# When results are read back, where the next pair's products begin, and how K products stand between scores, in a fused cross-attention and FFN kernel

## The chip, the cores and the metric

The kernel runs on one core of a Trainium2 chip. The metric is the device time of one execution in microseconds (us), the median of several runs. All data are fp32.

## The reference, cut to what matters

```python
# x (8,128,512), ctx (8,128,512); 32 heads of 128; INTER = 1376
h   = rmsnorm(layernorm(x)) * lnw
q, k, v = h @ w_q.T, ctx @ w_k.T, ctx @ w_v.T          # each (8,128,32,128)
score = einsum('bqhd,bkhd->bhqk', q, k) + position_bias
score = where(mask, score, -inf); p = where(mask, softmax(score), 0)
attn  = einsum('bhqk,bkhd->bqhd', p, v).reshape(8,128,4096)
x = x + layernorm(x) + attn @ w_out.T
n = layernorm(x)
x = x + ((silu((n @ Wg.T) * ag) * ((n @ Wu.T) * au)) @ Wd.T) * ad
```

## The kernel before

Every large product is done in seven half-size products instead of eight (the Strassen-Winograd form): a 2x2 block product needs seven products of blocks and of sums of blocks. `sums_a` (L222 to L225) and `sums_b` (L230 to L233) form the four sums of a left and of a right operand, each by four vector operations. The sums of weights are done by GpSimd (POOL), those of tokens and of attention results mostly by VectorE (DVE).

The program has these stages: K and V of head group 0, the Q products of all groups (queries go to DRAM), eight attention groups `g` of four heads, the output product, and the FFN (`mm_f` L916, `d` L995). The change lies in the attention stage and in the start of the output product.

**One attention step** (g, b) handles batch b, all four heads of the group:

- POOL adds the position bias and the mask into `s` (L332); the product of scores goes into the PSUM tile `sc` (L337, 8 matmul rows of the profile for four heads).
- DVE adds them (L340), takes the maximum (L342) and its negative `nmx` (L344); ScalarE (ACT) takes four exponentials with row sums (L347); DVE forms the reciprocal (`ri`, L354, L355), multiplies (L356), and transposes 32x32 blocks into `tt` (L372).
- SyncE's DMA queue (SP) writes `turned` (L374) to DRAM and reads it back as `pT` in four transfers (L379).
- Three steps later (`advance(3)`) TensorE (PE) multiplies `pT` with V into `av` (L395), ACT copies it to `aT` (L400), and ACT's DMA queue stores it in `att[g][b // 2]` (L401).

**Between the scores.** While group g's steps run, TensorE's remaining time goes to the K and V products of group g+1. They come from the generator `products` (`kv`, `project_T` L296, `project_V` L314, both through `seven`): each `next(products)` gives one product of one half (`t` = 0 or 1), followed by a copy on ACT (L270, L280) or an add on DVE (L275, L286) that takes the result out of its bank. The order of the seven is 2, 1, 6, 7, 4, 5, 3. Products 1, 6, 7 and 4 of one half share a bank, and each waits until the result of the one ahead is out. In group 0 three products stand ahead of the first scores, and then three or four between steps.

**The last group** (g = 7) has no next group. What is left of V's products is done in its first step, and from then on the output product of pair 0 (batches 0 and 1) stands between the scores: in step b the attention results `a` of group b are read back (`attended`, L608: on POOL's DMA queue for pair 0, on SP's for later pairs), DVE forms their sums `S_a`, and `out_products` multiplies with output weights `wo` of that group (L627, seven products, 28 matmul rows of the profile). `load_wo` fetches these weights (L588, L589, L596; 1 MB each on SP), and POOL forms their sums `T_o` right after. After the last step the remaining two `av` sets run, then pairs 1 to 3 of the output product, each in four PSUM banks.

**What sets the order.** A scheduler orders the instructions of each engine by its own estimates. What is issued through `InOrder` stays in the written order among its own kind; in the profile such instructions stand under L45. Until now that is TensorE in steps (0,0) to (0,3), TensorE and VectorE in the whole last group, and some other places. `acts` (18 slots of 4 KB per partition, tag "a"), `work`, `wpool` and `spool` hold the tiles, and a tile waits for the release of its slot. PSUM has two banks each for `sc`, `av`, `mm` (K and V products, later the first two out banks) and `pt`.

Of the kernel before, what the change touches and what calls it, by code (L numbers as in the profile page):

```python
# [10 lines left out]
F32 = mybir.dt.float32  # L11
U8 = mybir.dt.uint8
AF = mybir.ActivationFunctionType
ALU = mybir.AluOpType
# [3 lines left out]
P = 128  # L18
# [31 lines left out]
def xattn_ffn_kernel(  # L50
# [19 lines left out]
    nc = tc.nc  # L70
    B, S, D = x.shape
# [4 lines left out]
    GH = 4  # L76
    NG = H // GH
# [5 lines left out]
    HC = DC // 2  # L83
# [144 lines left out]
    def sums_b(eng, b11, b12, b21, b22, t1, t2, t4, eng3=None):  # L228

        eng.tensor_tensor(t1, b12, b11, SUB)  # L230
        eng.tensor_tensor(t2, b22, t1, SUB)
        (eng3 or eng).tensor_tensor(b12, b22, b12, SUB)
        eng.tensor_tensor(t4, b21, t2, SUB)  # L233
        return {1: b11, 2: b21, 3: b22, 4: t4, 5: t1, 6: t2, 7: b12}
# [89 lines left out]
        yield from seven(name, range(2), product, part, *banks)  # L324


    def probabilities(g, b, qT, kT, pb, between=None):

        cols = bass.ts(b, S)
        n = f"{g}_{b}"  # L330
        s = work.tile([P, GH, S], F32, tag="s", name=f"s_{n}", bufs=3)
        nc.gpsimd.tensor_tensor(  # L332
            s, pb, mneg[:, b : b + 1, :].to_broadcast([P, GH, S]), ALU.add
        )
        sc = ps.tile([P, GH, S], F32, tag="sc", name=f"sc_{n}")
        for j in range(GH):
            tensor.matmul(  # L337
                sc[:, j, :], qT[:, j, bass.ts(b % 2, S)], kT[j][:, cols], start=True, stop=True
            )
        vector.tensor_tensor(s, sc, s, ALU.add)  # L340
        mx = small.tile([P, GH], F32, tag="mx", name=f"mx_{n}")
        vector.tensor_reduce(mx, s, AX.X, ALU.max)  # L342
        nmx = small.tile([P, GH], F32, tag="nmx", name=f"nmx_{n}")
        vector.tensor_scalar(nmx, mx, FLOOR, -1.0, ALU.max, ALU.mult)  # L344
        sm = small.tile([P, GH], F32, tag="sm", name=f"sm_{n}")
        for j in range(GH):
            (InOrder(tc, nc.scalar) if (g, b) == (0, 0) else nc.scalar).activation(  # L347
                s[:, j, :], s[:, j, :], AF.Exp,
                bias=nmx[:, j : j + 1], accum_out=sm[:, j : j + 1],
            )  # L350
        if between:
            between()
        ri = small.tile([P, GH], F32, tag="ri", name=f"ri_{n}")
        vector.tensor_scalar_max(ri, sm, TINY)  # L354
        vector.reciprocal(ri, ri)  # L355
        vector.tensor_tensor(  # L356
            s, s, ri.unsqueeze(2).to_broadcast([P, GH, S]), ALU.mult
        )
        return s
# [46 lines left out]
    def advance(lag):  # L406
        while len(pend) > lag:
            attend(*pend.pop(0))
# [172 lines left out]

    def load_wo(g):
        src = woT[bass.ts(g, GW), :].rearrange("(c p) n -> p c n", p=P)
        if g == NG - 1:
            up, dn, t12, t4 = (
                acts.tile([P, 2, D], F32, tag="a", name=f"wo{g}_{k}") for k in range(4)
            )
            nc.sync.dma_start(up, src[:, :HC])  # L588
            nc.sync.dma_start(dn, src[:, HC:])  # L589
            t1, t2, t4 = (  # L590
                t.rearrange("p (c n) -> p c n", c=HC) for t in (t12[:, 0], t12[:, 1], t4[:, 0])
            )
        else:
            held = g in (2, 3, 4)
            w = (wpool if held else wos).tile([P, GH, D], F32, tag="w", name=f"wo{g}")
            nc.sync.dma_start(w, src)  # L596
            t = (spool if held else wos).tile(
                [P, 3, HC, HW], F32, tag="S" if held else "T", name=f"T_o{g}"
            )
            up, dn, t1, t2, t4 = w[:, :HC], w[:, HC:], t[:, 0], t[:, 1], t[:, 2]  # L600
        wo_t[g] = sums_b(
            nc.gpsimd, up[:, :, :HW], up[:, :, HW:], dn[:, :, :HW], dn[:, :, HW:], t1, t2, t4
        )

    def attended(g, i):
        a = acts.tile([P, 2, GH, S], F32, tag="a", name=f"a_{g}_{i}")

        (nc.sync if i else nc.gpsimd).dma_start(a, att[g][i])  # L608
        s = acts.tile([P, 3, HC, S], F32, tag="a", name=f"S_a{g}_{i}")
        return sums_a(  # L610
            vector, a[:, 0, :HC], a[:, 0, HC:], a[:, 1, :HC], a[:, 1, HC:],
            s[:, 0], s[:, 1], s[:, 2],
        )

    def by_product(banks):
        return {n: banks[k // 2][:, k % 2, :] for k, n in enumerate((1, 2, 6, 7, 4, 5, 3))}

    def out_products(i, order, banks, fetched):

        m = by_product(banks)  # L620
        for at, g in enumerate(order):
            sa = fetched.pop(g)
            if i and at + 1 < NG:
                fetched[order[at + 1]] = attended(order[at + 1], i)
            for k, n in enumerate((1, 2, 6, 7, 4, 5, 3)):
                for c in range(HC):
                    tensor.matmul(  # L627
                        m[n], sa[n][:, c, :], wo_t[g][n][:, c, :],
                        start=(g == order[0] and c == 0 and k % 2 == 0),
                        stop=(g == order[-1] and c == HC - 1), skip_group_check=True,  # L630
                    )
            yield


# [14 lines left out]
    for g in range(NG):  # L649
        kT, v = kvs.pop(g)  # L650
        pb = biases.pop(g)
        if g + 1 < NG:
            biases[g + 1] = load_bias(g + 1)
        if g + 2 < NG:
            kv_w[g + 2] = load_kv(g + 2)
        if g + 1 < NG:
            products = kv(g + 1, kvs)
        if g in (1, 2):
            load_wo(g - 1)
        if g == NG - 2:  # L660
            load_wo(2)
        if g == NG - 1:
            tensor, vector = InOrder(tc, nc.tensor), InOrder(tc, nc.vector)
            fetched = {}
        for b in range(B):
            if b % 2 == 0:
                qT = ahead.pop((g, b // 2))
                at = todo.index((g, b // 2)) + 2
                if at < len(todo):
                    ahead[todo[at]] = load_queries(*todo[at])  # L670

            if (g, b) == (0, 0):
                tensor = kv_tensor = InOrder(tc, nc.tensor)
                for _ in range(3):
                    next(products)
            if g == NG - 1:

                p = probabilities(
                    g, b, qT, kT, pb, lambda: fetched.update({b: attended(b, 0)})
                )  # L680
            else:
                p = probabilities(g, b, qT, kT, pb)
            pend.append((g, b, transpose_p(g, b, p), v))
            advance(3)

            if (g, b) != (0, 0):
                for _ in range(4 if b % 2 and (g < NG - 2 or b == 3) else 3):
                    next(products, None)
            if (g, b) == (0, 3):
                tensor = kv_tensor = nc.tensor  # L690
            if g == NG - 1:
                if b == 0:
                    proj.close()
                    wos = pools(outp)("wosB", 2, reuse_waits="tile")

                    first_banks = [
                        pl.tile([P, 2, HW], F32, tag=tag, name=f"m{k}_0")
                        for k, (pl, tag) in enumerate(2 * [(ps_mm, "mm")] + 2 * [(ps_tp, "pt")])
                    ]
                    first_out = out_products(0, list(range(NG)), first_banks, fetched)  # L700
                if b < NG - 4 or b == 5:
                    load_wo(b + 3 if b < NG - 4 else NG - 1)
                if b:
                    next(first_out)
    advance(2)
    next(first_out)
    advance(0)
    fetched[0] = attended(0, 1)
    tensor, vector = nc.tensor, nc.vector
    attn.close()  # L710


# [68 lines left out]
    for i in range(1, B // 2):  # L781
        last = i + 1 == B // 2
        order = [2, 3, 4, 5, 6, 7, 0, 1] if last else list(range(NG))
        banks = [ps.tile([P, 2, HW], F32, tag="m", name=f"m{k}_{i}") for k in range(4)]
        if i > 1:
            fetched[order[0]] = attended(order[0], i)
        for n, _ in enumerate(out_products(i, order, banks, fetched)):
            if n in (2, 3):
                norm2_T(*ys[n - 2])
        m = by_product(banks)  # L790
        first_residual(i)
        if last:
            outp.close()
            wts.close()
        else:
            residual(i, x1[i], m, banks)
            ys = norm2(i, x1[i])
# [276 lines left out]
```

## Time and profile before

| | |
|---|---|
| median of 3 runs | 1118.73 us (1117.19 to 1122.49) |
| profiled execution | 1120.01 us, span 1118.2 us |
| mean granted TensorE clock | 0.997 |
| PE busy | 1093.8 us, 98% of the span |
| POOL, DVE, ACT busy | 373.7, 571.4, 314.1 us |
| first attention group (first K product to first V product of the next group) | 247.33 to 282.81 us |
| last group, and pair 1 to its third group of heads | 682.72 to 781.59 us |

All times within the program are counted from the start of the span of the profiled execution. In a timeline row the first number is the start, the second the length of a group of instructions of one kind that follow each other, then engine, line, operation, output and inputs, shape and count; a bracket holds the idle time of the engine just before it and what released it. Matmuls are pipelined, so that rows that follow each other overlap a little. A table by stretches gives, for each stretch, its length, the busy time and number of instructions of PE, PEld (weight loads), DVE, ACT and POOL, then the granted clock of TensorE, the DMA engines' busy share and GB/s.

### The profile page before, as it was taken

Reading aid. Unit: us, or ns where it says so; the run is one execution under the profiler, and the core shown is the slowest. Engines: PE = TensorE matmul, PEld = TensorE weight load, DVE = VectorE, ACT = ScalarE, POOL = GpSimd, SP = SyncE. Lnnn points to the kernel's source line nnn. Section 1 sums busy time; section 2 is a strip of 40 time slices with the busy share of each in tenths; the row PEclk is TensorE's granted clock in tenths of the full one; section 3 lists DMA queues with packets and bytes.
Section 4 is the critical chain, followed back from the end, with each engine's and each line's share of the span. In section 5 each row is a group of like instructions: output and inputs, shape, how many; then the busy total and the mean of one; then the engine's idle time right before and its main releaser. Section 6 shows DMA issues by size and latency. Waiting matters only on the chain.

```text
span 1118.2 us, 13138 instructions
## 1 busy us (share of the span) xinstructions
PE 1093.8 (98%) x4526; PEld 775.1 (69%) x4526; DVE 571.4 (51%) x1122; ACT 314.1 (28%) x880; POOL 373.7 (33%) x386
## 2 busy tenths in 40 slices
PE   7999999998999999999999999998999999999998
PEld 4656666654868778685968778887888864444687
DVE  4664444436555565555555666643444333434732
ACT  2422211114444443434444344221000012223100
POOL 5283335535333333322311733620000316930010
PEclk9999999999999999999999999998999999999999
DMA  9113344448555555556545557664222512110011
GB/s 284 51 38 113 113 155 183 151 177 275 171 161 173 168 177 169 179 181 187 167 157 178 168 179 237 225 213 156 94 86 84 188 59 76 38 38 0 1 38 38
DMA packets 117538, 154.44 MB, mean 138 GB/s; under 512 B 12032, under 2 KB 71680, under 8 KB 117472
## 3 DMA queue, kind: packets, MB, share of 16 engines
q1 hardware_dynamic: 104416, 128.95, 36.2%
q10 hardware_dynamic: 11408, 18.88, 4.8%
q0 software_dynamic: 1648, 5.77, 1.6%
q8 instruction: 36, 0.59, 0.2%
q14 instruction: 30, 0.25, 0.1%
HBM read 101.14 MB, written 52.43 MB: 137 GB/s over the span
## 4 chain that ended last, share of the span: by engine, by line
PE 88%; DMA 4%; DVE 3%; POOL 2%; issue 1%; ACT 1%; SPq 0%; ACTq 0%; POOLq 0%; DVEq 0%
PE mm_v L314 16%; PE mm_k L296 14%; PE m L627 13%; PE mm_f L916 10%; PE mm_q L485 9%; PE d L995 6%; PE av L395 4%; PE sc L337 4%; PE ia_q L541 3%; PE ib_q L541 2%; PE mm_q L296 2%; DMA wo<-in_woT_dram 2%; DMA a<-att 1%; PE mm_k L45 1%; DMA wv<-in_wvT_dram 1%
## 5 line engine op out<-in xcount | busy, mean ns | idle before, releaser
L332 POOL TENSOR_TENSOR s<-pb,mneg 128x512 f32<-128x512 f32 x64 | 81.4, 1275 | 274.1 <-DVE tt L372 228.9
L314 PE MATMUL mm_v<-wv,ctx_sb 128*128 128x256 f32 x512 | 118.2, 379 | 1.4 <-DMA wv<-in_wvT_dram 1.4
L296 PE MATMUL mm_k<-ctx_sb,wk 128*128 128x512 f32 x224 | 105.0, 602 | 6.5 <-DMA wk<-in_wkT_dram 4.4
L347 ACT ACTIVATE s<-s,nmx 128x128 f32<-128x128 f32 x252 | 98.0, 390 | 44.6 <-DVE nmx L344 29.5
L314 PEld LDWEIGHTS mm_v<-wv,ctx_sb 128*128 128x128 f32 x512 | 94.5, 190 | 14.4 <-DMA wv<-in_wvT_dram 2.2
L314 PE MATMUL mm_v<-S_v,ctx_sb 128*128 128x256 f32 x384 | 86.6, 380 | 3.3 <-DVE v L45 1.7
L400 ACT COPY aT<-av 128x512 f32<-128x512 f32 x64 | 37.5, 587 | 183.2 <-PE av L395 142.1
L314 PEld LDWEIGHTS mm_v<-S_v,ctx_sb 128*128 128x128 f32 x384 | 71.9, 190 | 14.1 <-DVE v L45 2.3
L296 PE MATMUL mm_k<-ctx_sb,S_k 128*128 128x512 f32 x168 | 75.1, 592 | 0.0
L627 PE MATMUL m<-wo,a 128*128 128x256 f32 x300 | 74.3, 386 | 0.0
L337 PEld LDWEIGHTS sc<-k,q 128*128 128x128 f32 x416 | 58.7, 191 | 20.2 <-issue 18.2
L340 DVE TENSOR_TENSOR s<-sc,s 128x512 f32<-128x512 f32 x56 | 38.7, 691 | 65.3 <-PE sc L337 61.1
L296 PEld LDWEIGHTS mm_k<-ctx_sb,wk 128*128 128x128 f32 x224 | 40.4, 193 | 44.4 <-issue 34.8
L493 ACT COPY q<-mm_q 128x512 f32<-128x512 f32 x56 | 31.4, 588 | 121.5 <-PE mm_q L485 111.8
L627 PEld LDWEIGHTS m<-wo,a 128*128 128x128 f32 x300 | 57.6, 194 | 7.8
L545 DVE TENSOR_TENSOR q<-q,ia_q 128x256 f32<-128x256 f32 x84 | 34.9, 421 | 52.6 <-PE ia_q L541 51.7
L337 PE MATMUL sc<-k,q 128*128 128x128 f32 x416 | 59.0, 275 | 0.0
L296 PEld LDWEIGHTS mm_k<-ctx_sb,S_k 128*128 128x128 f32 x168 | 31.2, 190 | 35.4 <-issue 34.0
L395 PE MATMUL av<-pT,v 128*128 128x128 f32 x416 | 55.0, 275 | 0.0
L485 PE MATMUL mm_q<-hT,S_q 128*128 128x512 f32 x112 | 52.3, 592 | 0.0
L485 PE MATMUL mm_q<-hT,wq 128*128 128x512 f32 x112 | 52.3, 592 | 0.0
L395 PEld LDWEIGHTS av<-pT,v 128*128 128x128 f32 x416 | 50.6, 192 | 0.0
(251 smaller groups left out, 1940.7 us busy)
## 6 DMA issues: line engine op xcount, KB each, us to landing
queries<-q SPq DMA_DIRECT2D x32, 512.0 KB, 3.5
q<-queries SPq DMA_DIRECT2D x32, 512.0 KB, 4.8
turned<-tt SPq DMA_DIRECT2D x64, 256.0 KB, 2.1
pT<-turned SPq DMA_DIRECT2D x256, 64.0 KB, 2.6
att<-aT ACTq DMA_DIRECT2D x64, 256.0 KB, 3.1
a<-att SPq DMA_DIRECT2D x24, 512.0 KB, 3.3
wq<-in_wqT_dram SPq DMA_DIRECT2D x8, 1024.0 KB, 5.3
wk<-in_wkT_dram SPq DMA_DIRECT2D x7, 1024.0 KB, 6.2
```

Source lines behind the costliest of these rows:

```text
L296: kv_tensor.matmul(out, w[i][:, c, bass.ts(t, P)], src[i][:, c, :], start=(first and c == 0), stop=(c == HC - 1), skip_group_check=True,)
L314: kv_tensor.matmul(out[:, bass.ts(k, HW)], src[i][:, c, bass.ts(2 * t + k, S)], w[i][:, c, :], start=(first and k == 0 and c == 0), stop=( ...
L332: nc.gpsimd.tensor_tensor(s, pb, mneg[:, b : b + 1, :].to_broadcast([P, GH, S]), ALU.add)
L337: tensor.matmul(sc[:, j, :], qT[:, j, bass.ts(b % 2, S)], kT[j][:, cols], start=True, stop=True)
L340: vector.tensor_tensor(s, sc, s, ALU.add)
L347: (InOrder(tc, nc.scalar) if (g, b) == (0, 0) else nc.scalar).activation(s[:, j, :], s[:, j, :], AF.Exp, bias=nmx[:, j : j + 1], accum_out ...
L395: tensor.matmul(av[:, j, :], v[b // 2][:, b % 2, bass.ts(j, P)], pT[:, :, j, :], start=True, stop=True,)
L485: nc.tensor.matmul(m[t], w[i][:, c, bass.ts(t, P)], h_t[i][:, c, :], start=(i in (1, 5) and c == 0), stop=(c == HC - 1), skip_group_check= ...
L541: nc.tensor.matmul(m, a[n][i], b[n][i], start=i in (2, 1, 5), stop=True, skip_group_check=True)
L627: tensor.matmul(m[n], sa[n][:, c, :], wo_t[g][n][:, c, :], start=(g == order[0] and c == 0 and k % 2 == 0), stop=(g == order[-1] and c == ...
L916: nc.tensor.matmul(out, ws[t][n][:, c, :], h2_t[n][:, c, :], start=(first and c == 0), stop=(c == HC - 1), skip_group_check=True,)
L995: nc.tensor.matmul(out, lhs, rhs, start=bank not in started, stop=(i == NP - 1 or n == 8), skip_group_check=True,)
```

## The change

In the **first group** two K products instead of three stand ahead of the first scores; then three follow each of steps 0 to 5, and four steps 6 and 7 (before: none step 0, four the odd steps, three the other even ones). The weights wo0 and wo1 are still loaded in groups 1 and 2, but `load_wo` now keeps its loads in the written order on SP and gives back a function that does the sums; the sums are called in step 3 of groups 1, 2 and 6, in the written order on POOL.

In the **last group** the biases are added two steps ahead (`biased`), in the written order on POOL. The results `a` of pair 0 are read on SP's queue, in the written order, one step ahead of their sums (`come`); in steps 6 and 7 the results of pair 1 for groups 0 and 1 are read too. V's next product comes inside the softmax of step 0, ahead of the sums of `a`. The loads of wo3 to wo7 stand at the ends of steps 0 to 4, and their sums a step later. The sums of pair 1 for groups 0 and 1 are done by POOL. **Pair 1** begins in the two banks of `sc`: products 1, 2, 6 and 7 of group 0 stand between the last out product of pair 0 and `av_7_6`, those of group 1 between `av_7_6` and `av_7_7`; products 4, 5 and 3 of both follow behind `av_7_7`, in the banks of `av`.

The diff, cut to its core:

```diff
@@
+    def masked_bias(eng, g, b, pb):
+        s = work.tile([P, GH, S], F32, tag="s", name=f"s_{g}_{b}", bufs=3)
+        eng.tensor_tensor(s, pb, mneg[:, b : b + 1, :].to_broadcast([P, GH, S]), ALU.add)
+        return s
+
+    def probabilities(g, b, qT, kT, pb, between=None, s=None):
 
         cols = bass.ts(b, S)
         n = f"{g}_{b}"
-        s = work.tile([P, GH, S], F32, tag="s", name=f"s_{n}", bufs=3)
-        nc.gpsimd.tensor_tensor(
-            s, pb, mneg[:, b : b + 1, :].to_broadcast([P, GH, S]), ALU.add
-        )
+        if s is None:
+            s = masked_bias(nc.gpsimd, g, b, pb)
         sc = ps.tile([P, GH, S], F32, tag="sc", name=f"sc_{n}")
         for j in range(GH):
             tensor.matmul(
@@ 
 
     def load_wo(g):
         src = woT[bass.ts(g, GW), :].rearrange("(c p) n -> p c n", p=P)
+
+        sync = InOrder(tc, nc.sync)
         if g == NG - 1:
...
+        def sums(eng):
+            wo_t[g] = sums_b(
+                eng, up[:, :, :HW], up[:, :, HW:], dn[:, :, :HW], dn[:, :, HW:], t1, t2, t4
+            )
+        return sums
+
+    def load_att(g, i, eng):
         a = acts.tile([P, 2, GH, S], F32, tag="a", name=f"a_{g}_{i}")
-
-        (nc.sync if i else nc.gpsimd).dma_start(a, att[g][i])
+        eng.dma_start(a, att[g][i])
+        return a
+
+    def att_sums(g, i, a, eng):
         s = acts.tile([P, 3, HC, S], F32, tag="a", name=f"S_a{g}_{i}")
         return sums_a(
-            vector, a[:, 0, :HC], a[:, 0, HC:], a[:, 1, :HC], a[:, 1, HC:],
+            eng, a[:, 0, :HC], a[:, 0, HC:], a[:, 1, :HC], a[:, 1, HC:],
             s[:, 0], s[:, 1], s[:, 2],
         )
 
+    def attended(g, i):
+        return att_sums(g, i, load_att(g, i, nc.sync), nc.vector)
+
+    PRODUCTS = (1, 2, 6, 7, 4, 5, 3)
+
     def by_product(banks):
-        return {n: banks[k // 2][:, k % 2, :] for k, n in enumerate((1, 2, 6, 7, 4, 5, 3))}
-
-    def out_products(i, order, banks, fetched):
+        return {n: banks[k // 2][:, k % 2, :] for k, n in enumerate(PRODUCTS[: 2 * len(banks)])}
+
+    def out_product(g, sa, m, order, names=PRODUCTS):
+        for n in names:
+            for c in range(HC):
+                tensor.matmul(
+                    m[n], sa[n][:, c, :], wo_t[g][n][:, c, :],
+                    start=(g == order[0] and c == 0 and PRODUCTS.index(n) % 2 == 0),
+                    stop=(g == order[-1] and c == HC - 1), skip_group_check=True,
+                )
+
+    def out_products(i, order, banks, fetched, begun=0):
+
 
         m = by_product(banks)
-        for at, g in enumerate(order):
+        for names in ((4, 5), (3,)):
+            for g in order[:begun]:
+                out_product(g, fetched[g], m, order, names)
+        for g in order[:begun]:
+            del fetched[g]
+            yield
+        for at in range(begun, NG):
+            g = order[at]
             sa = fetched.pop(g)
             if i and at + 1 < NG:
                 fetched[order[at + 1]] = attended(order[at + 1], i)
-            for k, n in enumerate((1, 2, 6, 7, 4, 5, 3)):
-                for c in range(HC):
-                    tensor.matmul(
-                        m[n], sa[n][:, c, :], wo_t[g][n][:, c, :],
-                        start=(g == order[0] and c == 0 and k % 2 == 0),
-                        stop=(g == order[-1] and c == HC - 1), skip_group_check=True,
-                    )
+            out_product(g, sa, m, order)
             yield
 
 
...
-        if g in (1, 2):
-            load_wo(g - 1)
-        if g == NG - 2:
-            load_wo(2)
+        if g in (1, 2, NG - 2):
+            wo_sums = load_wo(min(g - 1, 2))
         if g == NG - 1:
             tensor, vector = InOrder(tc, nc.tensor), InOrder(tc, nc.vector)
-            fetched = {}
+            fetched, next_fetched = {}, {}
+            gpsimd, sync, wo_sums = InOrder(tc, nc.gpsimd), InOrder(tc, nc.sync), None
+            biased = [masked_bias(gpsimd, g, k, pb) for k in range(2)]
+            come = {(0, 0): load_att(0, 0, sync)}
         for b in range(B):
             if b % 2 == 0:
                 qT = ahead.pop((g, b // 2))
@@ 
 
             if (g, b) == (0, 0):
                 tensor = kv_tensor = InOrder(tc, nc.tensor)
-                for _ in range(3):
+                for _ in range(2):
                     next(products)
             if g == NG - 1:
 
-                p = probabilities(
-                    g, b, qT, kT, pb, lambda: fetched.update({b: attended(b, 0)})
-                )
+
+                if b + 2 < B:
+                    biased.append(masked_bias(gpsimd, g, b + 2, pb))
+                if b + 1 < B:
+                    come[b + 1, 0] = load_att(b + 1, 0, sync)
+                if b + 2 >= B:
+                    come[b + 2 - B, 1] = load_att(b + 2 - B, 1, sync)
+                if wo_sums:
+                    wo_sums = wo_sums(gpsimd)
+
+                def between():
+                    if b == 0:
+                        next(products)
+                    fetched[b] = att_sums(b, 0, come.pop((b, 0)), vector)
+
+                p = probabilities(g, b, qT, kT, pb, between, biased.pop(0))
             else:
                 p = probabilities(g, b, qT, kT, pb)
+                if g in (1, 2, NG - 2) and b == 3:
+                    wo_sums(InOrder(tc, nc.gpsimd))
             pend.append((g, b, transpose_p(g, b, p), v))
             advance(3)
 
-            if (g, b) != (0, 0):
-                for _ in range(4 if b % 2 and (g < NG - 2 or b == 3) else 3):
-                    next(products, None)
+            more = b > 5 if g == 0 else b % 2 and (g < NG - 2 or b == 3)
+            for _ in range(4 if more else 3):
+                next(products, None)
             if (g, b) == (0, 3):
                 tensor = kv_tensor = nc.tensor
             if g == NG - 1:
@@ 
                         for k, (pl, tag) in enumerate(2 * [(ps_mm, "mm")] + 2 * [(ps_tp, "pt")])
                     ]
                     first_out = out_products(0, list(range(NG)), first_banks, fetched)
-                if b < NG - 4 or b == 5:
-                    load_wo(b + 3 if b < NG - 4 else NG - 1)
+                if b < NG - 3:
+                    wo_sums = load_wo(b + 3)
                 if b:
                     next(first_out)
+                if b + 2 >= B:
+                    n = b + 2 - B, 1
+                    next_fetched[n[0]] = att_sums(*n, come.pop(n), gpsimd)
+
+    BEGUN = 2
+    second = list(range(NG))
+    second_banks = [ps.tile([P, 2, HW], F32, tag="sc", name=f"m{k}_1") for k in range(2)]
     advance(2)
     next(first_out)
+    for g in second[:BEGUN]:
+        out_product(g, next_fetched[g], by_product(second_banks), second, PRODUCTS[:4])
+        if g == 0:
+            advance(1)
     advance(0)
-    fetched[0] = attended(0, 1)
-    tensor, vector = nc.tensor, nc.vector
+    second_banks += [ps.tile([P, 2, HW], F32, tag="av", name=f"m{k}_1") for k in (2, 3)]
+    next_fetched[BEGUN] = attended(second[BEGUN], 1)
+    fetched = next_fetched
+    tensor, vector, gpsimd = nc.tensor, nc.vector, nc.gpsimd
     attn.close()
 
 
@@ 
     for i in range(1, B // 2):
         last = i + 1 == B // 2
         order = [2, 3, 4, 5, 6, 7, 0, 1] if last else list(range(NG))
-        banks = [ps.tile([P, 2, HW], F32, tag="m", name=f"m{k}_{i}") for k in range(4)]
-        if i > 1:
-            fetched[order[0]] = attended(order[0], i)
-        for n, _ in enumerate(out_products(i, order, banks, fetched)):
+        if i == 1:
+            banks, begun, ps.n = second_banks, BEGUN, 4
+        else:
+            banks = [ps.tile([P, 2, HW], F32, tag="m", name=f"m{k}_{i}") for k in range(4)]
+            fetched[order[0]], begun = attended(order[0], i), 0
+        for n, _ in enumerate(out_products(i, order, banks, fetched, begun)):
             if n in (2, 3):
                 norm2_T(*ys[n - 2])
         m = by_product(banks)
```

## The prediction

> **What bounds the kernel now.** I read the busy shares first, then the chain that ended last, then TensorE's waits, then stretches of the timeline.
>
> ```profile
> PE 1093.8 (98%) x4526; PEld 775.1 (69%) x4526; DVE 571.4 (51%) x1122; ACT 314.1 (28%) x880; POOL 373.7 (33%) x386
> PE 88%; DMA 4%; DVE 3%; POOL 2%; issue 1%; ACT 1%; SPq 0%; ACTq 0%; POOLq 0%; DVEq 0%
> ```
>
> TensorE is busy for 1093.8 of 1118.2 us, and the change takes no matmul away, so it can only save idle time and time at a lowered clock. TensorE's timeline shows both in two places. The bracket is the idle time before a row and its releaser. First group, then last group:
>
> ```profile
> 247.33 5.31 PE L45 MATMUL mm_k<-ctx_sb,wk 128*128 128x512 f32 x12
> ...
> 260.90 1.96 PE L45 MATMUL mm_k<-ctx_sb,wk 128*128 128x512 f32 x4 [1.32 <-ACT k L280]
> ...
> 268.85 1.98 PE L45 MATMUL mm_k<-ctx_sb,wk 128*128 128x512 f32 x4 [1.66 <-ACT k L280]
> ...
> 276.46 1.96 PE L45 MATMUL mm_k<-ctx_sb,S_k 128*128 128x512 f32 x4 [0.41 <-DVE k L286]
> 279.20 1.99 PE L45 MATMUL mm_k<-ctx_sb,S_k 128*128 128x512 f32 x4 [0.79 <-DVE k L286]
> ```
>
> ```profile
> 689.70 1.99 PE L314 MATMUL mm_v<-S_v,ctx_sb 128*128 128x256 f32 x8 [1.74 <-DVE v L45]
> ...
> 709.45 1.99 PE L45 MATMUL m<-wo,a 128*128 128x256 f32 x8 [0.31 <-DMA a<-att]
> 711.77 1.13 PE L45 MATMUL m<-T_o,S_a 128*128 128x256 f32 x4 [0.32 <-DVE S_a L45]
> ...
> 742.21 1.99 PE L45 MATMUL m<-wo,a 128*128 128x256 f32 x8 [0.58 <-DMA a<-att]
> ...
> 759.45 2.05 PE L45 MATMUL av<-pT,v 128*128 128x128 f32 x8 [3.10 <-DMA pT<-turned]
> 761.29 3.62 PE L627 MATMUL m<-wo,a 128*128 128x256 f32 x8
> ```
>
> First group: the waits sum to 4.18, and each restart adds about 0.25 (a four-instruction K product is 1.72 when it follows on, 1.96 to 1.99 in these rows). The stretch from 247.33 to the first V product at 282.81 is 35.5; its work is 14 K products x 1.72 + 5 score sets x 0.89 + 2 av sets x 0.89 = 30.3.
>
> Last group: the waits sum to 6.05. The last has a second price. The same eight matmuls (an av set) take 1.05 in other rows and 2.05 here, the next eight 3.62 for 1.89. The table by short stretches gives the granted clock:
>
> ```profile
> 757.00:758.00 1.00, 0.00 (x0) 0.00 (x0) 0.01 (x1) 0.00 (x0) 0.00 (x0) 1.00 1.10 203
> 758.00:759.00 1.00, 0.00 (x0) 0.00 (x0) 0.96 (x3) 0.00 (x0) 0.00 (x0) 0.75 0.95 255
> 760.00:762.00 2.00, 2.00 (x10) 1.91 (x9) 1.38 (x4) 0.47 (x1) 1.10 (x1) 0.50 0.99 389
> 766.00:768.00 2.00, 2.00 (x11) 1.77 (x10) 1.01 (x3) 0.00 (x0) 0.00 (x0) 1.00 0.02 7
> ```
>
> Last but two is the clock: 0.50 from about 758.5 to 765.3. The 84 out matmuls after it take 20.09 instead of 3 x 6.05 = 18.14, the av set 1 more: about 3 us. From 682.72 to 781.59, where pair 1's third group ends, is 98.9; the work is 88.7, so 10.2 is lost.
>
> **Last group, step by step.** Today a step's att results are fetched in the step that needs them (the 0.31 and 0.58 waits), and the DVE, held by them in its written order, has its softmax behind them: a DVE row at 742.19 shows `[7.56 <-DMA a<-att]`. That makes tt, turned and pT late and ends in the 3.10 wait. Afterwards each read stands one step ahead.
>
> - Waits 0.31, 0.32, 0.58: gone. Per step SP carries wo (1 MB; 6.4 to landing in the DMA table), one a (0.5 MB; 3.3 from SP), turned, four pT. I lay this chain out with the measured landings: a_6_0 is issued behind wo7 at 731.1, lands about 737.5, and its out product starts about 740.4. That is the tightest place.
> - The 3.10 wait: the eight out matmuls at half clock become two times four products of pair 1 (16 x 0.216 = 3.46 each) that stand before av_7_6 and av_7_7. out7 ends about 753.4, av_7_7 comes at about 761.5, pT_7_7 lands at about 754.5. Gain 3.10 + 0.25 + the 3 of clock.
> - The 1.74 wait: V product 5's second tile moves ahead of the DVE's att sums, so its add comes sooner. Gone.
> - New: a_0_0 is on SP behind pT_6_7. turned_6_7 lands about 684.2, the four issues take 1.8, so a_0_0 leaves at 686.1 and lands at 689.5 to 690.5. Behind its sums the DVE has ri, mult, tt and the two adds of V product 3, and the first out product needs the banks that these adds release: it starts at 693.4 to 694 instead of 691.5. Cost 1.9 to 2.4; I take 2.0.
> - Moved off: 8 reads leave POOL's queue (0.56 each on POOL) for SP (0.4 each; SP waits on landings most of the time). The sums of two groups of pair 1 go from DVE to POOL: 8 instructions, nearest row `T_d<-wd,T_d 128x256` at 0.81, 6.5 us in steps 6 and 7, where POOL has no more wo sums. Hidden: their products start at 753.4. Without that cover each step would be 3.2 late.
> - The wo loads come later than now (wo4 was issued at 681.0, now about 703) but their sums still end a step early. 0.
>
> Sum: 10.2 lost, less 2.0 kept = 8.2 gained.
>
> [...]
>
> **First group.** Two K products instead of three stand before the first scores, three after each, and the wo loads with their 8 POOL sums (261.28 to 272.0, ahead of late biases) leave for groups 1 and 2, where POOL and SP idle for most of a step and TensorE never waits. The copy waits shrink to two of about 0.6. But the order puts K product 1's first add, which frees the bank for product 6, behind the first softmax on the DVE. Scores end at 247.33 + 0.16 + 3.44 + 0.89 = 251.82; add, max and negation to 253.55; then exps and a table load: in the present trace nmx ends 255.73 and ri starts 258.78, 3.05 later. So ri at 256.60, the multiply ends 257.7, the add 258.4. TensorE ran out of work at 251.82 + 3.44 = 255.26: a new wait of 3.2. Carried on product by product, with the two 0.6 waits, the first V product is at 282.5 against 282.8: 0.3 gained, if the clock holds.
>
> Does it? The row: 3.10 idle halved the clock 2.15 after it began, and cost 3. Idle times up to 2.18 (at 27.2) did not. [...] As the window may lie otherwise, I take half of the row's price, 1.5: first group 1.2 lost. Both ends, 0.3 gained and 2.7 lost, stay in the range.
>
> **Sum:** 8.2 - 1.2 = 7.0 gained. The out0 wait of 2.0 may halve the clock too (idle 1.74 there didn't): 0.3 off for that. Net 6.7. The profiled execution is 1120.0 (span 1118.2), 1.3 over the median of 1118.7, inside its runs' spread of 5.3; so 1113.3 for it, 1112.0 as median.
>
> **Rivals.** 0.5% is 5.6 us, about what a measurement here can tell from no change.
>
> - A, as above: -5.5 to -8.5. For it: each removed wait has its releaser in the trace. 0.5.
> - B, the gain is mostly given back. The 3.2 wait halves the clock (3), a_0_0 lands later than 690.5 and TensorE's idle time there passes 2.2 and halves it too (2 + 1.5 more): 8.2 - 2.7 - 3 = 2.5 gained, -1 to -5. For it: turned_6_7 behind a 1 MB wo took about 6 in the present trace. Against: no wo is ahead of it now. 0.32.
> - C, slower: SP becomes the bound. turned takes 2.1 alone, but the one issued at 682.12, 1.1 behind a wo, let its pT out only at 688.41: about 6. Such a step on SP is 0.34 + 6 + 1.83 + 0.4 + 0.4 = 9.0 against 7.83, and pT's slack of 9.5 shrinks by 1.2 a step, which it outlasts. With a further 0.5 MB a in between turned may take 8, the step 11: 3.2 a step, slack gone after three steps, four late steps = 12 to 13; less 8.2, plus 1.2 of the first group: +5.5, up to +9. It decides from about 9.7 us a step on SP. 0.14.
> - D, the first group's order does as now and the att reads gain only the small waits: -1.5. The order as built speaks against it. 0.04.
>
> So faster 0.5, within 0.5% 0.34 (B, D and little of C), slower 0.16. The range: low 1108.5 (A with a free first group and a short out0 wait), high 1119.5, past B and D, leaving out C.
>
> **What would show it.** Right: an idle time of about 3 before an mm_k row near 258, released by DVE k L275 or its new line; no wait of 0.3 to 0.6 for a or S_a near 709 and 742; the last av rows with no idle time; four-product blocks of pair 1 near 754 and 758; pair 1's third group ending near 772 to 774. Wrong: no idle time near 255 (then more is gained), av rows in the last group that wait for pT, or a clock below 1 behind 255 or 693 (then less).

## The result, and the profile after

| | before | after |
|---|---|---|
| median | 1120.82 us (20 runs, 1116.74 to 1123.29) | 1120.86 us (20 runs, 1118.88 to 1125.71) |
| ratio after / before | | 1.0003, 95% interval 0.9995 to 1.0012 |
| profiled execution: span, clock | 1118.2 us, 0.997 | 1118.6 us, 0.995 |
| first group, first K product to first V product | 35.48 us | 35.35 us (247.23 to 282.58) |
| last group, first scores to the end of pair 1's third group | 98.9 us | 99.7 us (682.39 to 782.13) |

The change made no difference that can be measured; 6.7 us less were forecast, and the time lies above the range. Busy shares and chain of the page after:

```profile
PE 1094.5 (98%) x4526; PEld 776.0 (69%) x4526; DVE 584.2 (52%) x1114; ACT 313.9 (28%) x880; POOL 377.3 (34%) x386
PE 91%; DVE 4%; DMA 2%; ACT 1%; issue 1%; POOL 0%; SPq 0%; ACTq 0%; DVEq 0%
```

In the chain DMA went from 4% to 2%, POOL from 2% to 0% and DVE from 3% to 4%, and the time stayed: other waits, and time at a lowered clock, took the place of the old ones. TensorE's timeline of the changed kernel, first group, then last group:

```profile
258.34 1.96 PE L45 MATMUL mm_k<-ctx_sb,S_k 128*128 128x512 f32 x4 [3.19 <-DVE k L275]
...
265.18 1.98 PE L45 MATMUL mm_k<-ctx_sb,wk 128*128 128x512 f32 x4 [0.56 <-ACT k L280]
...
272.04 1.98 PE L45 MATMUL mm_k<-ctx_sb,S_k 128*128 128x512 f32 x4 [0.55 <-ACT k L280]
```

```profile
695.52 3.78 PE L45 MATMUL m<-wo,a 128*128 128x256 f32 x8 [4.22 <-DVE v L45]
699.10 1.87 PE L45 MATMUL m<-T_o,S_a 128*128 128x256 f32 x4
...
747.47 2.68 PE L45 MATMUL m<-wo,a 128*128 128x256 f32 x8 [2.12 <-DMA a<-att]
749.95 1.91 PE L45 MATMUL m<-T_o,S_a 128*128 128x256 f32 x4
```

All five old waits of the last group (1.74, 0.31, 0.32, 0.58, 3.10) are gone. Two new ones, at out0 and out6 (the out products of groups 0 and 6), have replaced them. Each runs into a slow clock, as the table by stretches shows (after the length come busy PE, PEld, DVE, ACT, POOL; the clock is the last number but two):

```profile
694.00:697.00 3.00, 1.48 (x4) 1.21 (x5) 2.93 (x6) 0.00 (x0) 1.27 (x1) 0.50 1.01 373
697.00:700.00 3.00, 3.00 (x9) 2.38 (x8) 2.67 (x7) 1.65 (x8) 1.17 (x1) 0.50 1.02 390
...
747.00:748.50 1.50, 1.03 (x5) 0.95 (x6) 1.10 (x2) 0.07 (x1) 1.50 (x2) 1.00 0.41 154
748.50:750.00 1.50, 1.50 (x6) 1.17 (x5) 1.50 (x2) 0.00 (x0) 1.50 (x2) 0.53 0.40 120
750.00:752.00 2.00, 2.00 (x6) 1.64 (x5) 1.90 (x6) 0.00 (x0) 0.32 (x1) 0.50 0.67 202
```

out0 takes from 695.52 to 704.26 = 8.74 and out6 from 747.47 to 755.28 = 7.81, where 6.05 is the full-speed length: 2.69 and 1.76 more, restart included. With the waits that is 4.22 + 2.69 + 2.12 + 1.76 = 10.8 lost, against 10.2 before.

Why out0 waited: the DVE's timeline.

```profile
691.58 0.42 DVE L45 TENSOR_TENSOR S_a<-a 128x256 f32<-128x256 f32 x1 [5.68 <-DMA a<-att]
...
693.46 0.69 DVE L45 TENSOR_TENSOR s<-s,ri 128x512 f32<-128x512 f32 x1
694.19 0.71 DVE L45 STREAM_TRANSPOSE tt<-s 128x512 f32<-128x512 f32 x1
694.82 1.25 DVE L45 TENSOR_TENSOR v<-v,mm_v 128x512 f32<-128x512 f32 x2
```

DVE stands idle for 5.68 until a_0_0 has landed. Then come four sums, the softmax's tail, the transpose, and only then the two V adds that free out0's banks; out0 starts as the first of them ends (694.82 + 0.69 = 695.51). TensorE had been free since 691.3.

Why out6 waited: SP's issues.

```profile
727.10 0.43 SPq L45 DMA_DIRECT2D wo<-in_woT_dram  x1
727.64 0.44 SPq L45 DMA_DIRECT2D a<-att  x1
731.79 0.33 SPq L377 DMA_DIRECT2D turned<-tt  x1
737.78 1.76 SPq L382 DMA_DIRECT2D pT<-turned  x4
739.59 1.00 SPq L45 DMA_DIRECT2D wo<-in_woT_dram  x2
740.63 0.47 SPq L45 DMA_DIRECT2D a<-att  x1
```

From turned to the first pT SP issues nothing for 6 us: turned must land first, and 1.5 MB issued at 727.1 and 727.6 are ahead of it. wo4 to wo7 were issued at 706.89, 717.05, 727.10 and 739.59, 10.1 to 12.5 apart, while TensorE's step takes 7.83. The read of group 6, behind wo7, left at 740.63.

### The profile page after: what moved, and what is told of

The parts are those of the page before. It is cut to its first block, busy times and chain, and to the rows that moved or that the text cites. A ratio compares the mean times of both kernels' runs of the same rounds, so it can differ in the third digit from the quotient of the medians.

```text
span 1118.6 us, 13124 instructions
## 1 busy us (share of the span) xinstructions
PE 1094.5 (98%) x4526; PEld 776.0 (69%) x4526; DVE 584.2 (52%) x1114; ACT 313.9 (28%) x880; POOL 377.3 (34%) x386
## 4 chain that ended last, share of the span: by engine, by line
PE 91%; DVE 4%; DMA 2%; ACT 1%; issue 1%; POOL 0%; SPq 0%; ACTq 0%; DVEq 0%
PE mm_v L314 16%; PE mm_k L296 14%; PE m L636 12%; PE mm_f L973 10%; PE mm_q L488 9%; PE d L1052 6%; PE av L398 4%; PE sc L340 4%; PE ia_q L544 3%; PE m L45 3%; PE ib_q L544 2%; PE mm_q L296 2%; PE mm_k L45 1%; DMA a<-att 1%; DMA wv<-in_wvT_dram 1%
## 5 line engine op out<-in xcount | busy, mean ns | idle before, releaser
L329 POOL TENSOR_TENSOR s<-pb,mneg 128x512 f32<-128x512 f32 x56 | 71.1, 1270 | 257.5 <-DVE tt L375 237.3
L636 PE MATMUL m<-wo,a 128*128 128x256 f32 x276 | 66.8, 379 | 0.0
L636 PEld LDWEIGHTS m<-wo,a 128*128 128x128 f32 x276 | 52.0, 190 | 6.8
```

The costliest lines, as they stand in the source:

```text
L329: eng.tensor_tensor(s, pb, mneg[:, b : b + 1, :].to_broadcast([P, GH, S]), ALU.add)
L636: tensor.matmul(m[n], sa[n][:, c, :], wo_t[g][n][:, c, :], start=(g == order[0] and c == 0 and PRODUCTS.index(n) % 2 == 0), stop=(g == ord ...
```

## The experiments

Each kernel was timed beside the kernel before on the same chip. The ratio is to that kernel, with its 95% interval. The chips differ from one experiment to another (the kernel before took 1120.82 to 1122.69 on them), so that two kernels are compared by their ratios, where 0.001 is 1.1 us, and not by their medians. The diffs are against the changed kernel and cut to their core.

| kernel | median us | ratio (interval) |
|---|---|---|
| changed kernel | 1120.86 | 1.0003 (0.9995 to 1.0012) |
| e1, a_0_0 on POOL's queue | 1113.91 | 0.9934 (0.9917 to 0.9950) |
| e2, a_6_0 ahead of wo7 | 1119.88 | 0.9988 (0.9979 to 0.9996) |
| e7, V adds ahead of the sums | 1120.13 | 0.9984 (0.9971 to 0.9997) |
| e5, K adds inside the first softmax | 1116.97 | 0.9958 (0.9944 to 0.9973) |
| u1, first group's spread undone | 1117.37 | 0.9952 (0.9933 to 0.9970) |
| c3, e1 + e5 + each a ahead of wo | 1112.45 | 0.9913 (0.9887 to 0.9939) |
| e8, c3 with pair 1 not begun | 1113.82 | 0.9930 (0.9907 to 0.9954) |
| e9, e1 without the wo sums | 1115.30 | 0.9940 (0.9921 to 0.9959) |
| c7, e1 + e5, wo on ACT's queue | 1110.02 | 0.9876 (0.9846 to 0.9907) |
| c6, e1 + e5, loads behind turned | 1106.70 | 0.9859 (0.9839 to 0.9880) |
| e12, c6 with pair 1 not begun | 1108.40 | 0.9887 (0.9870 to 0.9904) |
| e13, loads behind turned alone | 1117.87 | 0.9969 (0.9958 to 0.9981) |

**e1: the first read on another queue.**

```diff
-            come = {(0, 0): load_att(0, 0, sync)}
+            come = {(0, 0): load_att(0, 0, nc.gpsimd)}
```

> The changed kernel, with a_0_0 (the first attention results of the last group) read on POOL's queue as before the change; all other reads stay on SP. In the changed kernel out0 waited 4.22 us and then ran at half clock for another 2.45. Theory 1 (the late first read is the cause): a_0_0 lands before 685, the out0 wait falls to 0.5 or less, no half clock there, and out1 to out5 come 6 us earlier; the kernel is about 6 us (0.5%) faster if the later reads keep up. Rival (SP's queue as a whole is the limit in the last group, some 10 us a step, so that one repair only moves the wait): out6 still waits for a_6_0, which lands near 746 as it does now, its wait grows from 2.1 to 6 or 8, and the kernel stays within 2 us.

Measured: the wait at out0 and its slow clock are gone, and the stretch from the first scores to the end of pair 1's third group (the stretch, from here on) fell from 99.7 to 92.8. One read was worth 7. TensorE's timeline of e1 has new, smaller waits at out5 (the expectations of c3 and e9 call it out4):

```profile
731.32 1.99 PE L45 MATMUL m<-wo,a 128*128 128x256 f32 x8 [1.04 <-DMA a<-att]
734.08 1.10 PE L45 MATMUL m<-T_o,S_a 128*128 128x256 f32 x4 [0.76 <-DVE S_a L45]
```

So theory 1 holds for out0, and the rival has part of it: SP is late in e1 too.

**e7: the same late read, another order on DVE.**

```diff
                     if b == 0:
-                        next(products)
+                        for _ in range(3):
+                            next(products)
```

> The changed kernel, with the last two V products and their adds on DVE placed ahead of the DVE's sums of a_0_0, so that the banks of out0 are free before a_0_0 is there; a_0_0 itself comes as late as now (691.5). Theory 1b (a read that is 1 us late becomes a wait of 4.2 since the softmax tail and two adds stand behind it in the DVE's written order): out0 starts at 691.5 to 692.5 instead of 695.5, its wait is under 1, no half clock; 4 to 6 us earlier there. Rival (the read alone): out0 still waits 3 or more, since S_a of a_0_0 is needed as well.

Measured: a_0_0 was still late (the first sum waited for it until 691.97, which is 8.1 after the group's first scores; in the changed kernel 9.2), but out0 followed the av set ahead of it with no idle time, at 692.62. With the read 1.1 later still it would have waited some 0.5, by these numbers. So most of the 4.2 came through what the written order had put behind the sums. But the stretch fell only to 97.7, by 2.0. The waits came back at out4, with a slow clock behind it (3.15 instead of 1.89), and at out5:

```profile
726.61 3.15 PE L45 MATMUL m<-wo,a 128*128 128x256 f32 x8 [2.50 <-DMA a<-att]
737.97 1.96 PE L45 MATMUL m<-wo,a 128*128 128x256 f32 x8 [1.58 <-DMA a<-att]
```

**e2: one read ahead of its weights.**

```diff
+                if b == 4:
+                    come[6, 0] = load_att(6, 0, sync)
                 if b < NG - 3:
                     wo_sums = load_wo(b + 3)
```

> The changed kernel, with the read a_6_0 issued on SP just ahead of the two halves of wo7 instead of just behind them; nothing else moves. Theory 1 (a_6_0 is late because 1 MB of weights is ahead of it): a_6_0 lands near 743.5, the wait of 2.12 at out6 and the slow clock behind it (1.5 more) go, wo7 lands about 1 us later, 4 us ahead of its use: 3 to 4 us faster, the 4.22 at out0 stays. Rival (SP is late as a whole): wo7's sums come too late instead and out7 waits 2 or more for POOL; no gain.

Measured: the wait of 2.12 at out6 became 0.95, plus 0.36 for a pT, and no slow clock followed. The last group's stretch took 96.2, 3.5 less, as expected; out7 did not wait. In this profiled execution the clock halved in the first group and took 2.6 of it back (see the last section); by the ratios e2 is 1.7 faster than the changed kernel, less than the 3 to 4 expected.

**e5 and u1: the first group.** e5 puts the two adds that TensorE waits for ahead of the reciprocal; u1 puts the old spread back and keeps the wo sums out of the group.

```diff
+                vector = InOrder(tc, nc.vector)            # e5, step (0,0) only
...
-                p = probabilities(g, b, qT, kT, pb)
+                p = probabilities(
+                    g, b, qT, kT, pb,
+                    (lambda: [next(products) for _ in range(2)]) if (g, b) == (0, 0) else None,
+                )
```

> The changed kernel, with the two adds of K product 1 in the first step of the first group placed on DVE ahead of the reciprocal of the softmax instead of behind its multiply. Theory: the wait of 3.19 near 258 goes, the next wait for an ACT copy grows from 0.56 to about 1.1, the first V product starts near 279.7 instead of 282.58: 2.5 to 3 us faster. Rival (the exps' table load holds the copies on ACT, not the DVE's order): the wait moves to a copy and less than 1 us is gained.

> The changed kernel with the first group's spread of K products as before the change (three ahead of the first scores, none behind step 0, then three and four); the wo sums stay in steps 3 of groups 1 and 2, so POOL's biases are not late here. Theory (the first group's part exchanged waits of 4.2 for waits of 4.3): within 1 us of the changed kernel if the late biases played no part. Rival (the late biases caused the old waits of 1.3 and 1.7): those go, the first V product starts near 280 instead of 282.6, and this is 2 to 3 us faster than the changed kernel.

Measured in e5: the 3.19 is gone, the next wait is 0.92, and the first V product starts at 279.68, 2.9 earlier, as its theory had it. By the ratios e5 is 5.0 faster than the changed kernel (each interval is 1 to 2 us wide on either side); 0.9 more lies in the last group's stretch (98.8), and the trace of the changed kernel had no slow clock in its first group, which other executions had. In u1 the rival is right in the size. TensorE's timeline of u1:

```profile
260.71 1.96 PE L45 MATMUL mm_k<-ctx_sb,wk 128*128 128x512 f32 x4 [1.32 <-ACT k L280]
...
267.54 1.98 PE L45 MATMUL mm_k<-ctx_sb,wk 128*128 128x512 f32 x4 [0.55 <-ACT k L280]
...
279.80 3.62 PE L314 MATMUL mm_v<-wv,ctx_sb 128*128 128x256 f32 x16
```

The old spread has the V product at 279.80 once the eight POOL sums are away: of its old waits 1.66 became 0.55, and 0.41 and 0.79 went; 1.32, which the rival had named too, stayed. DVE's timeline of the kernel before shows two ways in which the sums had done it:

```profile
265.30 1.28 DVE L344 TENSOR_SCALAR nmx<-mx 128x4 f32<-128x4 f32 x1
...
273.29 0.69 DVE L340 TENSOR_TENSOR s<-sc,s 128x512 f32<-128x512 f32 x1 [1.65 <-POOL s L332]
```

The nmx of one step ran beside a POOL sum (265.28 to 266.55) and took 1.28, where it takes 0.17 in u1; the exps and the copy that ended the wait of 1.66 stand behind it. And the add at 273.29 waited for a bias that POOL began only at 271.98, behind its sums; the K adds that ended the waits of 0.41 and 0.79 stand behind that. (The loads of wo0 and wo1, 2 MB, left the first group together with the sums; no run separates the two.) So the first group's part was two edits that cancelled: moving loads and sums brought 2.8, the new spread took 2.7.

**c3 and e9: what makes SP slow?** c3 issues each a ahead of that step's wo load; e9 is e1 with POOL's sums of wo3 to wo7 left out.

```diff
+                if b + 2 < B:                               # c3, end of each step
+                    come[b + 2, 0] = load_att(b + 2, 0, sync)
                 if b < NG - 3:
                     wo_sums = load_wo(b + 3)
```

> The changed kernel with three edits: a_0_0 on POOL's queue (as in e1), the K adds inside the first softmax (as in e5), and in every step of the last group the read of a issued on SP just ahead of that step's wo load instead of just behind it. In e1 the reads a_4_0 to a_6_0 were issued right behind 1 MB of wo; a_4_0 took 7.5 us to land, DVE waited 3.69 for it, and its sums then ran beside POOL's wo sums at 1.2 to 1.5 each. Theory (order on SP): the reads land in 3 to 4, the waits of 1.04, 0.76, 0.30 and 0.30 at out4 and out5 go, the DVE's sums are over before POOL's begin; about 2.5 us less than e1 from that and 2.9 from the K adds: 1108 to 1109. Rival (SP's queue carries too much in any order): wo lands about 1.5 later, POOL's sums come later, and out6 or out7 waits for T_o or for pT; about 1111.

> e1, with the POOL sums of wo3 to wo7 left out (the products use the loaded blocks in their place), so that POOL has only the biases in the last group; loads and reads stay. Theory (a DVE operation with two inputs and a POOL operation hold each other up): the DVE's sums in steps 3 to 6 fall from 1.2 to 1.5 each to 0.42, tt of each step comes 3 to 4 us sooner, turned and with it the next wo and a too, and the waits at out4 and out5 go: about 2.5 us below e1. Rival (only the read behind wo): DVE still waits 3 us or more for a_4_0, and out4 still waits about 1.

Both theories failed. In c3 the stretch took 95.7, 2.9 more than in e1, with 2.58 for a pT, as its rival had it, 0.34 to 0.77 at three other places, and a slow clock at out7 (3.45 instead of 1.89); its first group gave e5's 2.9 as expected. SP's issues in c3 show why:

```profile
710.82 0.38 SPq L45 DMA_DIRECT2D a<-att  x1
711.24 0.44 SPq L45 DMA_DIRECT2D wo<-in_woT_dram  x1
711.74 0.49 SPq L377 DMA_DIRECT2D turned<-tt  x1
719.63 1.91 SPq L382 DMA_DIRECT2D pT<-turned  x4
```

turned now stands right behind 1.5 MB, and SP waits 7.4 for it. The next a and wo stand behind that wait. It is a loop, turned, pT, a, wo, turned, and the order of a and wo within it doesn't matter. In e9, DVE's timeline:

```profile
734.40 0.42 DVE L45 TENSOR_TENSOR S_a<-a 128x256 f32<-128x256 f32 x1 [7.45 <-DMA a<-att]
734.86 0.42 DVE L45 TENSOR_TENSOR S_a<-S_a,a 128x256 f32<-128x256 f32 x1
```

Each sum takes 0.42 without POOL's sums (1.22 to 1.48 in the same step of e1), but DVE waits 7.45 for the read, TensorE 1.62 at out5 and 1.40 at out6, and the kernel is no faster than e1 (ratios 0.9940 and 0.9934): the rival was right. The two engines do hold each other up (in that step of e1 the sums of POOL beside these took 1.45 and 1.44, and two like them, at 713.57 and 738.35, 1.27), and with reads that are this late it is not what sets the end.

**c6, c7 and e13: taking turned out of the loop.** c6 issues a and wo straight behind turned, ahead of the four pT, in the written order. There SP waits for a turned that has nothing large ahead of it, and pT, which lands behind wo, has three steps of slack.

```diff
-    def transpose_p(g, b, p):
+    def transpose_p(g, b, p, hook=None):
...
             d.rearrange("i c j n -> (i c) (j n)"), tt.rearrange("p j h c -> p (j h c)")
         )
+        if hook:
+            hook()
         pT = work.tile([P, 4, GH, BS], F32, tag="pT", name=f"pT_{n}", bufs=4)
...
+            def loads():
+                nonlocal wo_sums
+                if b + 2 < B:
+                    come[b + 2, 0] = load_att(b + 2, 0, sync)
+                if b < NG - 3:
+                    wo_sums = load_wo(b + 3)
```

> c3, with the order on SP changed once more: in each step of the last group the read of a and the load of wo are issued straight behind turned and ahead of the four pT, and all of these in the written order. In c3 they stood behind pT and so just ahead of the next turned, which then took 7 to 9 us to land; SP waits for it before it can issue pT, so that its step is about 10.9 us against TensorE's 7.83. Theory (turned queued behind 1.5 MB is what makes SP slow): turned lands in 2 to 3 us with pT alone ahead of it, SP's step follows TensorE's 7.83, no wait for a or pT of more than 0.5 is left in the last group: 4.5 us of waits and about 1.5 of slow clock less than c3, 1106 to 1107. Rival (the bytes are too many in any order): pT lands 7 us later than now behind wo and av waits for it, or wo's sums come late; no gain over c3.

> The changed kernel with a_0_0 on POOL's queue and the K adds inside the first softmax, and with the loads wo3 to wo7 on ACT's DMA queue; the reads of a stay on SP where the change put them. Theory (it is the order within SP's queue): turned is no longer behind wo and lands in 2 to 4 us, reads of a in 3 to 5, no wait of more than 0.5 for a, S_a or pT in the last group; 1106 to 1108. Rival (the 16 DMA engines are shared, so wo slows turned from another queue too): turned still takes 6 or more, out4 or out5 waits as in e1, 1110 to 1111.

> The changed kernel with c6's order on SP alone: in each step of the last group a and wo behind turned and ahead of pT. a_0_0 stays on SP behind pT_6_7, and the first group stays as changed. Theory (two separate causes: a_0_0 late at out0, and SP's slow step at out6): the wait of about 4 at out0 with its slow clock stays, the wait of 2.1 at out6 and the 1.5 behind it go; about 4 us faster than the changed kernel. Rival (one cause, SP's slow step): out0's wait shrinks as well, 8 or more faster.

TensorE's waits in c6 from 240 to 800, then SP's issues of a step:

```profile
PE mm_k L45 <- ACT k L280: 1.5, 2, 0.9
```

```profile
713.39 0.34 SPq L45 DMA_DIRECT2D turned<-tt  x1
713.84 0.38 SPq L45 DMA_DIRECT2D a<-att  x1
714.26 0.46 SPq L45 DMA_DIRECT2D wo<-in_woT_dram  x1
715.74 1.99 SPq L45 DMA_DIRECT2D pT<-turned  x4
```

The last group has no wait of TensorE at all: from its first scores (679.71) to 768.34 is 88.6, the length of the work alone (88.7 in the prediction's count). turned to pT is 2.35 here. The DMA tables of 700 to 752, first c3, then c6, show the trade: turned sooner, pT later and harmless.

```profile
turned<-tt SPq DMA_DIRECT2D x5, 256.0 KB, 6.7
pT<-turned SPq DMA_DIRECT2D x20, 64.0 KB, 2.0
```

```profile
turned<-tt SPq DMA_DIRECT2D x6, 256.0 KB, 3.1
pT<-turned SPq DMA_DIRECT2D x24, 64.0 KB, 4.3
```

c6 beats both kernels: 1106.70, ratio 0.9859, and c3 with the same bytes on the same queue (0.9913) by more than the intervals: the order on SP is the cause. c7 moves wo to ACT's queue instead. Its stretch takes 92.7, no less than e1's 92.8: turned still takes 4.7 with no wo ahead of it on SP, and waits of 2.1 remain, at out4, out5 and one av set. It does not tell how much of that is wo's transfers on the other queue, since the move held up ACT as well: in one step nmx was ready at 707.85 and ri, which stands behind the exps, began only at 712.70, after 3.39 of idle time on DVE that ended with the exps; in the same step of e1 it was 707.62 and 709.50, after 0.43. Its ratio of 0.9876 overlaps with c6's, and one of its four runs took 1104.80.

e13 separates the two causes in the changed kernel: out6 no longer waits, out0 still does.

```profile
695.40 3.78 PE L45 MATMUL m<-wo,a 128*128 128x256 f32 x8 [3.92 <-DVE v L45]
```

Its stretch takes 95.5 instead of 99.7, which is out6's 2.12 + 1.76 and 0.3 of out0's. By the ratios it is 3.8 faster than the changed kernel: the theory's "about 4".

**e8 and e12: was it worth beginning pair 1 early?** Both leave that part out.

```diff
-    BEGUN = 2
+    BEGUN = 0
```

> c3, with pair 1 not begun early: its first two reads and sums come after the last step, as before the change, and av_7_6 and av_7_7 follow each other. Theory (the early products cover the way of pT_7_7): av_7_7 waits 2 to 4 us for pT_7_7, the clock falls in part, and pair 1's first products wait for their a; 3 to 7 us slower than c3. Rival (with all else in time pT_7_7 is in time too): within 1 us of c3.

> c6 (no wait left in the last group), with pair 1 not begun early, as in e8. In e8 this cost about 1 against c3, where SP was late anyhow. Theory (with SP in time, the early products still cover the way of the last pT and of pair 1's first reads): av_7_7 comes about 7 us earlier than in c6 and waits 0.5 to 2 for pT_7_7, and pair 1's first group waits 1 to 2 for its own read; 1.5 to 4 slower than c6. Rival (no cover is needed once SP is in time): within 1 of c6.

Against c3 nothing can be told (1113.82 and 1112.45, overlapping intervals; and the trace of c3 has a slow clock at out7 that e8's has not). Against c6, e12's last av set waits:

```profile
749.15 1.89 PE L639 MATMUL m<-wo,a 128*128 128x256 f32 x8
750.88 0.59 PE L639 MATMUL m<-T_o,S_a 128*128 128x256 f32 x2
753.66 1.13 PE L45 MATMUL av<-pT,v 128*128 128x128 f32 x8 [2.19 <-DMA pT<-turned]
```

The stretch took 91.1 instead of 88.6; the two ratios differ by 3 us, and their intervals overlap. But the first two rows are pair 1's: with nothing written there, the scheduler put ten of its matmuls ahead of the last av set by itself. So e12 prices the written beginning at some 2.5 against a shorter one, and not against none. From the end of the av set before (749.3) to this one are 4.4 us; before the change they were 3.1. So the last pT comes no sooner behind its neighbour for all of c6's order, and only the cover makes the wait shorter. No slow clock followed the wait of 2.19 here: the eight matmuls behind it took 1.13 (2.05 at half clock in the kernel before), and the mean clock of this execution is 1.0. Pair 1's own first read caused no wait, other than expected.

## Why the prediction was wrong

The step that failed is the arrival of two reads on SP's queue. The sum priced out0 at 2.0 and out6 at nothing; they cost 6.9 and 3.9, which uses up the 8.2 forecast for the last group. What the change was to remove it did remove: the mechanism was right there, and two terms were mis-sized.

- **Right:** TensorE as the bound; all five old waits gone; the first group step by step (a new wait of 3.2 behind the K add: 3.19; two copy waits of about 0.6: 0.56 and 0.55; first V product at 282.5: 282.58).
- **First group's clock, 1.5 of 3 taken:** half of one row's price, taken because "the window may lie otherwise"; no run shows such a window, nor a price of 1.5 by itself. What the runs showed in its place: in six profiled executions with that wait the group took 35.35 three times (the changed kernel, e1, e9) and 36.75, 37.05 and 37.97 in e7, e13 and e2, so 0 or 1.4 to 2.6 more, 0.95 on average. As a mean 1.5 was a fair size; in the profile after, the price was 0.
- **"Cost 1.9 to 2.4; I take 2.0" at out0: the first term mis-sized.** It measured 4.22 + 2.69. The chain behind the read was right (3.9 from its landing to out0), and the arrival was not: the four pT issues took 3.00 for 1.8, and a_0_0 took 4.4 to land for the 3.3 of the table, with a read of q, a_1_0 and wo3 issued within 1.8 behind it. 691.5 instead of 689.5 to 690.5 drew the idle time out past 694.0, where the clock halved. 0.3 was set aside for that, 2.4 it cost. Rival B had named just this, a landing behind 690.5 and a halved clock, at 3 to 3.5 more; it came to 4.6 more.
- **"Waits 0.31, 0.32, 0.58: gone" with a slack of 2.9 at a_6_0: the second term mis-sized.** It measured 2.12 + 1.76, since a_6_0 left at 740.63, not 731.1. The sum laid SP's chain out with turned at 2.1, the median of a program in which few of them have a wo ahead. Here it took 4.4 in the median of 700 to 752, and 6 in the step shown above. Rival C named this mechanism and its point, 9.7 us a step, and SP passed it (10.1 to 12.5). C expected pT to give way first; the read of a did, and e13 prices it at 4, not at 12.
- **The 3.10 wait, 6 to 7 with its clock:** it went, as forecast. What the early beginning alone is worth stays open: e12 shows 2.5 against a shorter one.
- **The DVE's sums beside POOL's, no term in the sum:** none was needed for the order of e1, as e9 shows, although they ran at 1.22 to 1.49 in several steps of e1 (0.42 in e9). The kernel before had it too: two of them took 1.38 and 1.49 at 694.8 to 697.5, beside wo sums. And in the first group before, nmx beside a POOL sum took 1.1 longer, and that is what the wait of 1.66 lost in u1.
- **"Leave for groups 1 and 2" with no price and no gain:** the move of the wo loads and sums was worth 2.8 by u1. The sum put the first group's gain down to the spread, which lost as much.

The 8.2 forecast for the last group, less what was not foreseen (2.2 + 2.4 at out0, 3.9 at out6), leaves -0.3; the stretch is 0.9 longer than before.

## What to carry to other kernels

Where a queue issues in order and one of its transfers must land before the next can be issued, put the large loads behind that transfer, not ahead of it: the same bytes cost 7 us of waiting and slow clock in one order (c3, turned 6.7 to landing) and none in the other (c6, 3.1). A landing time from a table belongs to what was ahead of the transfer there; lay the queue out with the new neighbours. And where an engine has a written order, a late read holds up all that stands behind it: out0's wait was 4.2 with the adds behind the sums and none with them ahead. So put work that others wait for ahead of an instruction that may wait.

## What the runs showed of the hardware

The length of a gap alone does not tell whether the clock halves. In the changed kernel half clock followed a wait of 2.12 (745.35 to 747.47), from 748.6 on, a microsecond after TensorE had gone on; in the kernel before none followed one of 2.18 (27.2 to 29.4). One of 3.19 had none behind it in three executions of six and had it in the others. e2's row behind the same wait, 3.75 long where the changed kernel's is 1.96:

```profile
260.04 3.75 PE L45 MATMUL mm_k<-ctx_sb,S_k 128*128 128x512 f32 x4 [3.19 <-DVE k L275]
```

In the profile after, the changes lie at 694.0, 700.8, 748.6 and 752.0: half clock lasted 6.8 behind the wait of 4.22 and 3.4 behind that of 2.12. In the profile before it lasted 6.8 (758.5 to 765.3), behind the wait of 3.10. What decides whether a gap of 2 to 3.2 is followed by half clock was not shown: no run moved one wait by small steps to test it. So such a gap has a range here and not one price: the 3.19 cost nothing in three executions, and 1.4, 1.7 and 2.6 in the others.
